# Depthwise taps of 128 channels moved from VectorE to TensorE as 32x32 diagonal tiles, with a new order of issue

## The chip, the core and the metric

The kernel runs on one NeuronCore of a Trainium2 chip. Its engines work side by side and are synchronised by semaphores: TensorE (matmuls, PE in the profile; PEld is its weight loading), VectorE (DVE), ScalarE (ACT), GpSimd (POOL) and SyncE (SP, which here only issues DMAs). Here each engine's instructions are given in a fixed order by the program. Matmuls read the on-chip memory SBUF and write PSUM; VectorE and ScalarE read both.

The metric is the time of one execution on the device in microseconds, the median of several runs. The profile is one execution, recorded instruction by instruction.

## What is computed

64 images of 96 channels by 56x56 pixels pass through a convolution block, a Fourier attention and a feed-forward part. Cut to what matters here (`bn` are folded batch norms):

```python
# convolution block, per image
out = silu(bn(einsum('bchw,oc->bohw', x, expand_w)))          # 96 -> 192 channels
out = channel_shuffle(shift_groups(out), groups=4)             # each quarter shifted by one pixel
dw  = bn(conv(out, dw_w, 3x3, feature_group_count=192))        # depthwise: 9 taps a channel
idb = bn(out * id_w)
out = silu(bn(dw + idb))
se  = sigmoid(grouped_1x1(relu(grouped_1x1(mean(out)))))       # one gate a channel
out = silu(bn(einsum('bchw,oc->bohw', out * se, proj_w)) + x)  # 192 -> 96, plus x
# attention on tokens t = [3136, 96]
h = relu(bn(layernorm(t) @ w1.T))
X = fft(h, axis=tokens); xr, xi = relu(...X...), relu(...X...)
t = t + bn(ifft(xr + 1j * xi).real @ w2.T)
# feed-forward in 8-bit floats
t = t + qlinear(relu(qlinear(layernorm(t), W1, b1)), W2, b2)
```

A depthwise tap multiplies every pixel of a channel by one number of that channel and adds it, shifted by up to one pixel, to the result. All nine taps of the 192 channels are the work that the change moves.

## The kernel before

The 192 middle channels lie in two arrays: `e_a` holds 128 channels of the whole image, one channel a partition; `e_b` holds the other 64 channels twice, the upper half of the image in partitions 0 to 63 and the lower half in 64 to 127. A depthwise pass `i` covers 28 rows: 0 and 1 are the halves of `e_a`, 2 is all of `e_b`. Every tap is one VectorE instruction over 128x1568 numbers:

```python
    x_buf = [const.tile([CP, PAD, PAD], F32, name=f"x_{i}") for i in range(2)]
    t_buf = [const.tile([CP, NPIX + 8], F32, name=f"t_{i}") for i in range(2)]
    # ... (cut)
    d_buf = const.tile([128, 3 * HH, HW], F32, name="d")

    def depthwise(b, i):
        # ... (cut)
        h, r0 = divmod(i, 2)
        e = e_b if h else e_a
        dst = d_buf[:, i * HH : (i + 1) * HH, :]
        for n, tap in enumerate((4, 0, 1, 2, 3, 5, 6, 7, 8)):
            dy, dx = divmod(tap, 3)
            win = e[:, dy + r0 * HH : dy + r0 * HH + HH, dx : dx + HW]
            w = taps[:, h, tap : tap + 1]
            if n == 0:
                nc.vector.tensor_scalar(dst, win, w, None, ALU.mult)
            else:
                nc.vector.scalar_tensor_tensor(dst, win, w, dst, ALU.mult, ALU.add)
            yield

    def mid_silu(b, i, cvs):                       # ScalarE, with the sums for the gates
        # ... (cut)
        nc.scalar.activation(
            dst, dst, AF.Silu, bias=mid_b[:, i // 2 : i // 2 + 1], accum_out=cvs[b][:, i : i + 1]
        )
        yield

    def project(b, cvs):
        # ... (cut)
        for j in range(HW // PJ):                  # 8 groups of 7 rows
            # ... (cut)
            ps = psb.tile([CP, PJ, HW], F32, tag="psb", name="ps_pj")
            nc.tensor.matmul(ps, lhsT=eye, rhs=xi[:, ...], start=True, stop=False)            # adds x
            nc.tensor.matmul(ps, lhsT=pw[:, 0, :], rhs=d_buf[:, r0 : r0 + PJ, :], start=False, stop=False)
            nc.tensor.matmul(
                ps, lhsT=pw[:, 1 + half, :], rhs=d_buf[:, HW + rb : HW + rb + PJ, :], start=False, stop=True
            )
            nc.scalar.activation(tv[:, :, r0 : r0 + PJ], ps.rearrange("p a b -> p b a"), AF.Silu, bias=pj_sh)
            yield
        if b + 2 < NB:
            load_x(b + 2)

    def deviations(b):                             # of the layer norm before the attention
        def squares(g):
            cen = psb.tile([C, 4 * CP], F32, tag="psb", name="ps_c")
            nc.tensor.matmul(cen, lhsT=center, rhs=t[:, g * 4 * CP : (g + 1) * 4 * CP], start=True, stop=True)
            sqs[g] = work.tile([C, 4, CP], F32, tag="sq", name="sq")
            nc.scalar.activation(sqs[g], cen.rearrange("p (k f) -> p k f", f=CP), AF.Square)
        def variances(g):
            # ... (cut)
            for k in range(4):
                nc.tensor.matmul(var[:, k : k + 1], lhsT=sq[:, k, :], rhs=mean_m, start=True, stop=True)
            nc.vector.tensor_scalar(v[:, js], var, 1e-5, None, ALU.add)
            nc.gpsimd.tensor_tensor(rs[:, js], v[:, js], mhalf[0:CP, 0:4], ALU.pow)
        # ... (cut)
```

PSUM is split into two pools: `psa`, two tiles of two banks for the attention, and `psb`, four tiles of one bank for everything else.

The order of issue is worked out as the program is built. The attention of image b (`mixing`, with six stages: `ps_w` from `w1`, `ps_f` twice, `ps_w` from `w2`, `ps_i` twice) is the main line. Between its steps the other parts ("sides") are put in: the feed-forward of image b-1, and the convolution of images b+1 and b+2. `PLAN` says at which points of the main line, in units of its own, a side begins and ends:

```python
PLAN = {
    "mixing": (22.3, 18.0, 30.7, 18.0, 12.0, 23.2),
    "ffn": (0.0, 63.5),
    "expand_a": (1.2, 20.0),
    "depthwise_2": (8.4, 36.3),
    # ... (cut)
    "excitation": (42.0, 44.0),
    "project": (60.0, 86.0),
    # ... (cut)
    "deviations": (87.0, 110.4),
    "silu_1": (115.9, 118.2),
}
```

The first two images' convolution is done part after part ahead of the first attention.

## Time and profile before

Three runs took 9521.79, 9529.6 and 9544.45 us. The profiled execution has a span of 9482.8 us.

| | busy us | share of the span |
|---|---|---|
| TensorE, matmuls | 8133.7 | 86% |
| VectorE | 6389.5 | 67% |
| ScalarE | 4790.4 | 51% |
| GpSimd | 2240.6 | 24% |

| operation | us of one, mean | count |
|---|---|---|
| tap, `scalar_tensor_tensor` on 128x1568 | 1.85 | 1536 |
| silu of a pass, 128x1568 | 1.61 | 192 |
| projection matmul, 128x392 (each recorded twice) | 0.49 a record | 3072 records |
| silu of the projection, 112x392 | 0.62 | 512 |
| load of half of x, 588 KB, to landing | 8.3 (median) | 128 |

The granted TensorE clock averages 0.898 of full speed. How to read the profile: lines of the kernel are given as L with a number; `out<-in` are the program's names of what an instruction writes and reads. A float32 matmul is recorded as two matmuls and two weight loads. The recorded lengths of matmuls overlap, because they are pipelined, so the distance from start to start is the better measure. In the list of waits each line reads: who waited, for whom, how long in total, how often, and the longest. A wait put down to "issue" is time in which an engine waited for nothing that the profile shows.

### The profile page before, as it was taken

What the parts mean: (1) busy time and instruction counts of PE and PEld (TensorE: products, weight loads), DVE (VectorE), ACT (ScalarE), POOL (GpSimd) and SP (SyncE); (2) the same over time, 40 slices, a digit from 0 to 9 for tenths busy, and PEclk for the clock granted to TensorE, in tenths of its full rate; (3) what the DMA queues carried; (4) which work ended last, traced back from release to release, by engine and by line L of the source; (5) the groups of instructions that cost most, each with busy time, mean ns of one, the idle gap of its engine ahead of it and who ended that gap; (6) DMA issues with size and microseconds to landing.
All of it is one profiled execution on the core that took longest, in us unless ns stands there. A gap on an engine that the chain in (4) does not pass through costs nothing.

```text
span 9482.8 us, 263604 instructions
## 1 busy us (share of the span) xinstructions
PE 8133.7 (86%) x118530; PEld 6030.7 (64%) x118530; DVE 6389.5 (67%) x9034; ACT 4790.4 (51%) x9099; POOL 2240.6 (24%) x1360
## 2 busy tenths in 40 slices
PE   5888888888888888888888888888888888888887
PEld 3666666666666666666666666666666666666666
DVE  6667666666666766676666766666666666676764
ACT  2455454454554545545545545455455454554545
POOL 0222222222222222222222222222222222222221
PEclk8988999898888999999989989889998898888988
DMA  2111111111101111111111111111110111111100
GB/s 40 17 22 16 19 21 16 20 17 17 22 15 19 17 19 21 17 18 21 17 17 22 16 19 18 17 21 17 17 22 14 20 17 17 22 16 19 18 13 15
DMA packets 411399, 177.45 MB, mean 19 GB/s; under 512 B 366323, under 2 KB 409707, under 8 KB 410011
## 3 DMA queue, kind: packets, MB, share of 16 engines
q1 hardware_dynamic: 408508, 155.59, 13.0%
q8 instruction: 930, 15.24, 0.7%
q10 hardware_dynamic: 1264, 3.48, 0.1%
q0 software_dynamic: 496, 1.50, 0.1%
q14 instruction: 201, 1.64, 0.1%
HBM read 82.62 MB, written 77.07 MB: 17 GB/s over the span
## 4 chain that ended last, share of the span: by engine, by line
PE 67%; DVE 13%; ACT 9%; issue 6%; POOL 5%; DMA 0%; POOLq 0%; ACTq 0%; DVEq 0%
PE ps_f L490 8%; PE ps_i L608 7%; PE ps_c L417 5%; PE ps_i L590 5%; POOL rs L650 5%; PE ps_v L426 4%; PE ps_w L468 4%; PE ps_pj L395 4%; PE ps_w L555 4%; PE ps_pj L396 4%; PE ps_pj L397 3%; DVE d L343 3%; PE ps_f L524 3%; ACT h L684 3%; DVE buf_h L475 3%
## 5 line engine op out<-in xcount | busy, mean ns | idle before, releaser
L343 DVE SCALAR_TENSOR_TENSOR d<-e_a,taps,d 128x1568 f32<-128x1568 f32 x1024 | 1892.0, 1848 | 14.3
L428 POOL TENSOR_TENSOR rs<-v,mhalf 112x4 f32<-112x4 f32 x448 | 1060.1, 2373 | 2650.7 <-DVE v L427 2589.6
L700 POOL TENSOR_TENSOR o<-t,o 112x448 f32<-112x448 f32 x448 | 587.6, 1312 | 2921.7 <-DVE o L698 2921.7
L650 POOL TENSOR_TENSOR rs<-v,mhalf 112x4 f32<-112x4 f32 x448 | 582.8, 1301 | 1637.1 <-DVE v L649 1637.1
L343 DVE SCALAR_TENSOR_TENSOR d<-e_b,taps,d 128x1568 f32<-128x1568 f32 x512 | 943.4, 1843 | 0.5
L427 DVE TENSOR_SCALAR v<-ps_v 112x4 f32<-112x4 f32 x448 | 72.0, 161 | 1281.0 <-PE ps_v L426 1270.3
L490 PEld LDWEIGHTS ps_f<-f_tab,buf_h 128*64 128x64 f32 x24576 | 747.3, 138 | 163.5 <-DVE buf_h L475 57.2
L490 PE MATMUL ps_f<-f_tab,buf_h 128*64 128x58 f32 x24576 | 797.8, 223 | 40.0 <-DVE buf_h L475 40.0
L676 ACT CAST y<-ps_h 128x448 f16<-128x448 f32 x1344 | 723.9, 539 | 148.8 <-PE ps_h L674 130.2
L684 ACT CAST h<-y 128x448 fp8e5<-128x448 f16 x1344 | 770.4, 573 | 0.3 <-DVE y L681 0.3
L681 DVE TENSOR_SCALAR y<-y,qb 128x448 f16<-128x448 f16 x1344 | 649.1, 487 | 154.6 <-ACT y L676 135.4
L590 PE MATMUL ps_i<-inv_tab,buf_g 112*32 112x56 f32 x24576 | 482.4, 253 | 285.7 <-issue 284.8
L468 PE MATMUL ps_w<-w1c,t 112*64 112x96 f32 x14336 | 708.0, 250 | 0.0
L468 PEld LDWEIGHTS ps_w<-w1c,t 112*64 112x64 f32 x14336 | 611.6, 137 | 139.3 <-issue 117.0
L426 PEld LDWEIGHTS ps_v<-mean_m,sq 96*112 96x112 f32 x3584 | 516.2, 213 | 281.4 <-issue 257.2
L608 PE MATMUL ps_i<-r_tab,buf_h 64*64 64x56 f32 x14336 | 676.1, 276 | 1.0 <-ACT buf_h L597 1.0
L590 PEld LDWEIGHTS ps_i<-inv_tab,buf_g 112*32 112x32 f32 x24576 | 439.1, 139 | 339.8 <-issue 293.0
L608 PEld LDWEIGHTS ps_i<-r_tab,buf_h 64*64 64x64 f32 x14336 | 647.9, 189 | 5.0 <-ACT buf_h L597 1.1
L475 DVE SCALAR_TENSOR_TENSOR buf_h<-ps_w,rs_full 128x768 f32<-128x768 f32 (+1 forms) x512 | 437.3, 854 | 254.8 <-PE ps_w L468 245.8
L690 PE MATMUL ps_o<-h,q 128*112 128x448 fp8e5 x1344 | 421.3, 393 | 213.1 <-ACT h L684 213.0
L597 ACT COPY buf_h<-ps_i 128x896 f32<-128x896 f32 x192 | 174.0, 906 | 787.8 <-PE ps_i L590 787.8
L417 PE MATMUL ps_c<-t,center 112*96 112x448 f32 x896 | 553.2, 706 | 11.6 <-issue 10.9
(159 smaller groups left out, 14740.5 us busy)
## 6 DMA issues: line engine op xcount, KB each, us to landing
x<-in_x SPq DMA_DIRECT2D x128, 588.0 KB, 8.3
out_dram<-o SPq DMA_DIRECT2D x896, 84.0 KB, 1.9
l_tab<-in_tab_l ACTq DMA_DIRECT2D x1, 1624.0 KB
r_tab<-in_tab_r ACTq DMA_DIRECT2D x1, 1568.0 KB
t<-dev_t SPq DMA_DIRECT2D x64, 7.0 KB, 1.8
t<-dev_t SPq DMA_DIRECT2D x64, 5.2 KB
ex_row_p<-in_expand_row POOLq DMA_DIRECT2D x1, 336.0 KB, 4.2
s_p<-in_bn POOLq DMA_DIRECT2D x1, 288.0 KB, 4.0
```

The costliest lines, as they stand in the source:

```text
L343: nc.vector.scalar_tensor_tensor(dst, win, w, dst, ALU.mult, ALU.add)
L417: nc.tensor.matmul(cen, lhsT=center, rhs=t[:, g * 4 * CP : (g + 1) * 4 * CP], start=True, stop=True)
L426: nc.tensor.matmul(var[:, k : k + 1], lhsT=sq[:, k, :], rhs=mean_m, start=True, stop=True)
L428: nc.gpsimd.tensor_tensor(rs[:, js], v[:, js], mhalf[0:CP, 0:4], ALU.pow)
L468: nc.tensor.matmul(ps[hc * 64 : hc * 64 + 64, k, 0:C], lhsT=t[:, n0 : n0 + 64], rhs=w1c[:, hc * C : hc * C + C], start=True, stop=True,)
L475: nc.vector.scalar_tensor_tensor(h_v[:, :, d * NJ + j0 : d * NJ + j0 + n], ps[:, 0:n, 0:C].rearrange("p b c -> p c b"), 0.0, rs_full[:, d, ...
L490: nc.tensor.matmul(ps[r * 64 : r * 64 + 64, k, 0 : 2 * NK], lhsT=buf_h[:, n0 : n0 + 64], rhs=f_tab[:, r, :], start=True, stop=True,)
L590: nc.tensor.matmul(ps[p0 : p0 + 32, k, 0:HW], lhsT=u_v[:, oh * 48 + o, :], rhs=inv_tab[:, r, :], start=True, stop=True,)
L608: nc.tensor.matmul(ps[pr, bk, k, 0:HW], lhsT=buf_h[pr, n2 * 48 : n2 * 48 + 64], rhs=r_tab[pr, n2, :], start=True, stop=True,)
L650: nc.gpsimd.tensor_tensor(rs, v, mhalf[0:CP, 0:4], ALU.pow)
L676: nc.scalar.copy(y16, ps)
L684: nc.scalar.copy(held[i // 3][:, i % 3, :], held.pop(("y", i)), saturate=False)
```

## The change

The taps of the 128 channels of `e_a` become matmuls with diagonal weights: for each tap and each group of 32 channels a 32x32 matrix with the taps on its diagonal. The 128x128 array is used as 16 tiles. Row tile r reads channels 32r to 32r+31; column tile j works on another group of seven rows of the image. The four row tiles write four different PSUM banks, so half an image (four row groups) takes all four `psb` tiles, and the nine taps are summed in PSUM. ScalarE then applies the silu out of PSUM. The taps of `e_b` stay on VectorE. The purpose is to take work off VectorE and to use a TensorE array that has idle parts in such small products.

After that, a partition of `d_buf` holds 32 channels of one row group, so the projection is done in row tiles of 32 rows, four at a time, with the `e_b` part in two row tiles of 64. The identity matmul that added x is replaced by an addition on VectorE in PSUM. The variances of the layer norm take the form used in the feed-forward part: pixels on partitions, and a reduction on VectorE in place of matmuls with a column of 1/96. There is one x buffer (two before) and there are three t buffers (two before). A single schedule orders all images; a side that holds all four `psb` tiles keeps others out until it is done ("hold"), and cannot start within the first part of the feed-forward ("part").

```diff
 PLAN = {
-    "mixing": (22.3, 18.0, 30.7, 18.0, 12.0, 23.2),
-    "ffn": (0.0, 63.5),
-    "expand_a": (1.2, 20.0),
...
+    "mixing": (16.9, 18.0, 30.0, 18.0, 12.0, 19.7),
+    "ffn": (112.9, 176.9),
+    "expand_a": (-139.2, -120.0),
+    "expand_b": (-114.4, -95.4),
+    "depthwise_0": (-118.2, -110.2),
+    "depthwise_1": (-100.1, -97.9),
+    "last_taps": (-97.5, -76.2),
+    "last_silu": (-89.9, -63.3),
+    "excitation": (-71.5, -57.0),
+    "project": (-66.5, -42.2),
+    "deviations": (-40.0, -17.7),
 }
...
+    def depthwise(b, i, cvs):
...
+        pss = [psb.tile([128, PJ, HW], F32, tag="psb", name="ps_d") for _ in range(4)]
+        for tap in range(9):
+            dy, dx = divmod(tap, 3)
+            for j in range(4):
+                r0 = start_row(i, j) + dy
+                for r in range(4):
+                    pr = slice(r * 32, r * 32 + 32)
+                    nc.tensor.matmul(
+                        pss[r][j * 32 : j * 32 + 32],
+                        lhsT=diag[pr, tap, :],
+                        rhs=e_a[pr, r0 : r0 + PJ, dx : dx + HW],
+                        start=tap == 0,
+                        stop=tap == 8,
+                    )
+            if tap % 3 == 2:
+                yield "hold"
+        for r in range(4):
+            nc.scalar.activation(
+                d_buf[:, i, r], pss[r], AF.Silu, bias=mid_b[:, r : r + 1], accum_out=sums[:, i * 4 + r : i * 4 + r + 1]
+            )
+        yield
...
     def project(b, cvs):
...
+        for i in range(2):
+            pss = [psb.tile([CP, PJ, HW], F32, tag="psb", name="ps_pj") for _ in range(4)]
+            for g in range(4):
+                for j in range(4):
+                    pr = slice(j * 32, j * 32 + 32)
+                    nc.tensor.matmul(pss[j], lhsT=pw[pr, g, :], rhs=d_buf[pr, i, g], start=g == 0, stop=False)
+                if g == 1:
+                    yield "hold"
+            for j in range(4):
+                pr = slice(j % 2 * 64, j % 2 * 64 + 64)
+                r0 = (2 * i + j // 2) * PJ
+                nc.tensor.matmul(pss[j], lhsT=pw[pr, 4, :], rhs=d_last[pr, r0 : r0 + PJ, :], start=False, stop=True)
+            yield "hold"
+            for j in range(5):
+                if j < 4:
+                    r0 = start_row(i, j)
+                    nc.vector.tensor_tensor(
+                        pss[j], pss[j], xi[:, r0 + 1 : r0 + 1 + PJ, 1 : HW + 1], ALU.add
+                    )
+                if j:
...                      # silu of row group j - 1 into t, on ScalarE
+                yield None if j == 4 else "hold"
+        load_x(b + 1)
...
         def squares(g):
-            cen = psb.tile([C, 4 * CP], F32, tag="psb", name="ps_c")
-            nc.tensor.matmul(cen, lhsT=center, rhs=t[:, g * 4 * CP : (g + 1) * 4 * CP], start=True, stop=True)
...
+            cen = psb.tile([CP, 4, 128], F32, tag="psb", name="ps_c")
+            for k in range(4):
+                n0 = (g * 4 + k) * CP
+                nc.tensor.matmul(cen[:, k, 0:C], lhsT=t[:, n0 : n0 + CP], rhs=center, start=True, stop=True)
...
         def variances(g):
-            for k in range(4):
-                nc.tensor.matmul(var[:, k : k + 1], lhsT=sq[:, k, :], rhs=mean_m, start=True, stop=True)
...
+            nc.vector.tensor_reduce(v[:, js], sqs.pop(g), AX.X, ALU.add)
...
     # feed-forward: the second product of a row group is issued one step later
-            j, m = divmod(i - 5, 3)
-            if i >= 5 and m == 0 and j < NCH:
+            j, m = divmod(i - 6, 3)
+            if i >= 6 and m == 0 and j < NCH:
                 second(j)
...
+    # what a side waits for: (part, how many images back, steps)
+    SIDES = {
+        "expand_a": (7, (("project", 1, None),)),
+        "depthwise_0": (4, (("expand_a", 0, None),)),
+        "last_taps": (9, (("expand_b", 0, None),)),
+        "project": (14, (("excitation", 0, None), ("ffn", NT, None))),
+        "deviations": (10, (("project", 0, None), ("mixing", 1, 8))),
...
```

The times in the new plan count from the start of the image's own attention, so -139.2 lies in the attention of image b-2. The gate now also uses a form that needs no halving, and the excitation takes nine sums in place of three.

## The prediction

> **What bounds the kernel now.** I read the engines' shares first, then the stretches, the waits of TensorE, the groups of the parts that change, and last a timeline of one period. The page and the stretch from 1000 to 9000 us (busy time of each engine, then granted clock):
>
> ```profile
> PE 8133.7 (86%) x118530; PEld 6030.7 (64%) x118530; DVE 6389.5 (67%) x9034; ACT 4790.4 (51%) x9099; POOL 2240.6 (24%) x1360
> PE 67%; DVE 13%; ACT 9%; issue 6%; POOL 5%; DMA 0%; POOLq 0%; ACTq 0%; DVEq 0%
> ...
> 1000.00:9000.00 8000.00, 6950.09 (x101502) 5155.75 (x101503) 5445.07 (x7692) 4102.07 (x7797) 1931.86 (x1153) 0.90 0.14 18
> ```
>
> TensorE is busy 86.9% of the stretch. The first matmul of the attention stage (the first `ps_w` of each image) returns every 146.7 us (median of 63 distances). So one image costs 127.4 us of busy TensorE, 99.8 of VectorE, 75.2 of ScalarE; TensorE idles 19.2 us. The second line, the chain that ended last, shows the same: TensorE two thirds, VectorE next. What TensorE waits for (total us, times, longest):
>
> ```profile
> PE ps_i L590 <- issue: 284.8, 55, 5.9
> PE ps_dev L434 <- DVE dev L432: 229.1, 128, 3.2
> PE ps_o L690 <- ACT h L684: 213.0, 272, 1.5
> PE ps_x L665 <- DVE xt L656: 175.8, 199, 2.0
> PE ps_se L372 <- ACT red L367: 146.5, 64, 2.3
> ```
>
> Divided by 64: 4.4, 3.6, 3.3, 2.7 and 2.3 us an image. Those on `dev` and `xt` come from VectorE's queue, where one tap holds 1.85 us:
>
> ```profile
> L343 DVE SCALAR_TENSOR_TENSOR d<-e_a,taps,d 128x1568 f32<-128x1568 f32 x1024 | 1892.0, 1848 | 14.3
> L343 DVE SCALAR_TENSOR_TENSOR d<-e_b,taps,d 128x1568 f32<-128x1568 f32 x512 | 943.4, 1843 | 0.5
> L341 DVE TENSOR_SCALAR d<-e_a,taps 128x1568 f32<-128x1568 f32 x128 | 131.8, 1030 | 11.1 <-PE ps_pj L396 7.7 <-ACT e_a L298 3.4
> L648 DVE TENSOR_REDUCE v<-sq 112x4 f32<-112x384 f32 x448 | 243.8, 544 | 23.8 <-ACT sq L641 23.8
> L618 DVE SCALAR_TENSOR_TENSOR t<-ps_i,bn2c_b,t 112x392 f32<-112x392 f32 x512 | 296.3, 620 | 159.0 <-PE ps_i L608 157.3
> ```
>
> The timeline (start, length, engine, line) gives what a float32 matmul costs; each is recorded as two:
>
> ```profile
> 4081.47 0.96 PE L297 MATMUL ps_ea<-x,ex_w 112*32 112x448 f32 x8
> ...
> 4005.55 1.52 PE L312 MATMUL ps_eb<-x,ex_b 112*32 112x392 f32 x16
> ...
> 4014.27 0.82 PE L396 MATMUL ps_pj<-d,pw 128*112 128x392 f32 x2
> 4014.93 0.82 PE L397 MATMUL ps_pj<-d,pw 128*112 128x392 f32 x2
> ...
> 4052.29 2.02 PE L590 MATMUL ps_i<-inv_tab,buf_g 112*32 112x56 f32 x74 [5.15 <-issue]
> ```
>
> A full-width matmul of 392 columns takes 0.66 us from start to start. Four in four column tiles (`ps_ea`, 448 columns) take 0.9 us together, eight of `ps_eb` in two rounds 1.46 us: 0.73 us for a round of four. Within a round the records start 6 to 7 ns apart. The last line shows the stall put down to "issue": 5.15 us with nothing to wait for, 10 us after the two loads of x (588 KB each) were issued at 4037.51. I take it that TensorE's own instructions arrive late behind those loads; the profile does not prove it.
>
> **What the Trainium skill says.** "TensorE: Matmul & The Clock Gate", Part 3 (packing small matmuls), gives 10.6x for 16 tiles of 32x32 at 512 columns, tiles starting some 4 ns apart. The trace agrees as far as it goes: four column tiles side by side, and two row tiles of 64 (`ps_w` from `w2b`: eight matmuls of 96 columns in 0.96 us, 0.12 each, against 0.195 for full-height ones). Sixteen appear nowhere in it. "TensorEngine Tiling (Array Packing)", Restrictions and Gotchas, wants different row tiles in different PSUM banks; the change does that, which is why one depthwise step takes four `psb` banks. Its Key Properties say a change of tiling drains TensorE; here that is the 0.1 to 0.15 us by which a batch's first interval is longer. Part 1 of the first page says the array's clock falls after idle windows; the trace grants 0.90, and the same eight `ps_ea` records take 1.72 us at 175.49 and 0.96 at 178.89.
>
> **The change, part by part, us per image.**
> VectorE loses the taps of the first 128 channels: (1892.0+131.8)/64 = -31.6. It gains eight additions of x, at the 0.62 of the like-sized `t` update +5.0, and seven reductions at 0.544 (+3.8). 99.8 becomes 77.
> ScalarE: two silus of 1.61+0.19 become eight of about 0.5+0.19 (`e_b`, 392 columns from PSUM, takes 0.498): +1.9; the rest cancels. 75 becomes 77.
> TensorE, from busy time by tile in the same stretch (us of 8000, divided by 54.5 images):
> 1. Old projection, 926.2: -17.0.
> 2. Variances: `ps_c` 469.8 and `ps_v` 397.6 go, -15.9. The new form is that of `ps_n` in the feed-forward part, 390.2: +7.2.
> 3. Taps: 2 halves x 9 taps x 16 matmuls of 392 columns. If 16 tiles run together, a tap is one round: 18 x 0.73 = 13.1.
> 4. New projection: per half, 16 matmuls of 32 rows in four row tiles (4 rounds) and 4 of 64 rows in two (2 rounds); 12 x 0.66 = 7.9, with drains 8.5. The identity matmul that added x is gone.
> Sum: 127.4 - 17.0 - 15.9 + 7.2 + 13.1 + 8.5 = 123.3. TensorE's work shrinks by only 4 us; the larger gain must come from its idle time.
>
> Idle, 19.2 now. `dev` 3.6 -> 1: the plan puts the remaining taps (-97.5 to -76.2) where no deviations (-40.0 to -17.7) run. `xt`, with the smaller releasers of `ps_x`, 3.2 -> 2: those taps come after the first part of the feed-forward. `ps_o` 3.3 -> 0.5: it is issued one step later. `ps_se` 2.3 -> 0.5: four steps spread over 14 units instead of 2. Issue 4.4 -> 3: x is now loaded in the middle of the `ps_w` stage, whose instructions are sparser than those of `ps_i`. Remainder 1.5. New: two depthwise halves and two projection halves each need all four `psb` banks empty and keep the other side work out; I put 1.5 us on each, 6 in all. Sum 14.5.
>
> Period 123.3+14.5 = 137.8, 8.9 less. The mean of the 63 periods is 1% under the median now, so 63 x 136.4 = 8593. Before the first period: 172.7 us now, of which two images' taps fill much; with one image at the start I expect 115. After the last start 157 now, 155 then. 8863 in the profile; measured times lie 0.5% above it (9529.6 against 9482.8): 8907. The plan's own period falls from 124.2 to 114.6, 7.7%; applied to 145.3 this gives 63 x 134.1 + 270 = 8718, or 8760 measured. I take 8840.
>
> **Rivals.**
> A. Sixteen tiles do not overlap, only four: 72 rounds x 0.73 = 52.6 instead of 13.1. TensorE 163, period 177, total about 11,500. For it: no such pattern in the trace. Against: four column tiles and two row tiles do overlap, and records can follow at 6.5 ns, so 32 fit in a round. 6%.
> B. The four-bank holds cost 4 to 5 us each, not 1.5: every hold waits for the last evictions of other work and ends behind four silus in ScalarE's queue. Idle is then 26, period 149, total about 9600. Against: attention has its own two PSUM buffers and can fill the gap. 8%.
> C. The single x, e and d buffers make the convolution a closed loop: expand to projection spans 97 of the plan's 114.6 units, at 1.2 us a unit 116 us, plus 10 us for loading x: 126. Under 138, but with 12 us of slack; were it exceeded, the period would be set there, at 140 to 145, total 9000 to 9300. 12%.
> D. Everything fits better than I allow, idle 8 us, and a busier TensorE keeps a higher clock: period 129, total about 8400. 15%.
>
> **Range and chances.** 8840, 8450 to 9300 for eight in ten: the low end is near D, the high end takes in most of C. Over 2% faster means under 9339: all but A, B and a little of C, 0.88. Within 2% 0.05, slower 0.07.
>
> **What would show it.** TensorE busy about 123 us an image; 16-tile rounds of 0.66 to 0.75 us; VectorE near 77; the wait on `dev` gone; projection near 8.5. Wrong if a tap round takes over 1 us (A), if `ps_d` and `ps_pj` wait for ScalarE over 10 us an image (B), or if `ps_ea` waits for x (C).

## The result and the profile after

| | before | after | ratio to before |
|---|---|---|---|
| median time, us | 9525.7 (9517.7 to 9544.5, 4 runs) | 9241.4 (9232.7 to 9243.3, 4 runs) | 0.9697, interval 0.968 to 0.9714 |
| profiled span, us | 9482.8 | 9238.1 | |
| period of the first `ps_w`, us (median) | 146.7 | 143.0 | |
| TensorE busy in a period, us | 127.4 | 126.9 | |
| VectorE busy in the span | 67% | 52% | |

The change gains 3.0%, 284 us; I had forecast 8840, a gain of about 690. The profiled spans differ by 245 us: 63 periods that are 3.4 us shorter in the mean (211), a start shorter by 27 (with the convolution of one image ahead of the first attention, in place of two) and a tail shorter by 6. Two lines of the page of the changed kernel (engines' shares; the chain that ended last) and the stretch from 1000 to 9000 us (busy time of each engine, then granted clock):

```profile
PE 8110.8 (88%) x159362; PEld 6129.3 (66%) x159362; DVE 4801.2 (52%) x8793; ACT 4804.3 (52%) x9806; POOL 1771.3 (19%) x1360
...
PE 72%; ACT 13%; DVE 9%; issue 5%; DMA 0%; POOL 0%; ACTq 0%; POOLq 0%; SPq 0%; DVEq 0%
...
1000.00:9000.00 8000.00, 7099.70 (x139856) 5371.24 (x139851) 4167.61 (x7622) 4200.86 (x8582) 1548.95 (x1176) 0.94 0.14 19
```

VectorE has lost a quarter of its work and its share of the chain has fallen from 13% to 9%; TensorE's has risen from 67% to 72%. The granted clock has risen from 0.90 to 0.94. What TensorE waits for (total us, times, longest):

```profile
PE ps_se L406 <- ACT red L400: 335.4, 64, 5.8
PE ps_h L726 <- ACT y L728: 143.8, 66, 2.3
PE ps_i L644 <- issue: 126.2, 56, 4.4
PE ps_x L719 <- DVE xt L710: 104.8, 73, 1.8
PE ps_o L744 <- ACT h L738: 98.3, 124, 1.7
```

The wait on `dev` is gone from the list. The one on `red`, 2.3 us an image before, stands first with 5.2. The groups of the parts that changed (busy us, mean ns of one, idle before):

```profile
L359 PE MATMUL ps_d<-e_a,diag 32*32 32x392 f32 x36864 | 1040.5, 497 | 0.0
L382 DVE SCALAR_TENSOR_TENSOR d_last<-e_b,taps,d_last 128x1568 f32<-128x1568 f32 x512 | 954.1, 1864 | 12.6 <-ACT e_b L334 9.9
...
L438 PE MATMUL ps_pj<-d,pw 32*112 32x392 f32 x4096 | 470.6, 506 | 33.8 <-DVE pw L421 32.7 <-ACT t L454 0.6
...
L480 DVE TENSOR_REDUCE v<-sq 112x4 f32<-112x384 f32 x448 | 247.7, 553 | 1011.6 <-ACT sq L476 1006.6
...
L444 PE MATMUL ps_pj<-d_last,pw 64*112 64x392 f32 x1024 | 201.5, 512 | 0.0
```

Divided by 64: taps on TensorE 16.3 us an image, projection 10.5, taps left on VectorE 14.9 without the first, and 3.9 for the reductions that VectorE has gained (3.8 forecast).

Where in the image the time went is seen when a period is cut at the first matmul of each attention stage (medians; us, TensorE's busy part behind the slash):

| stage, by its matmuls | before | after |
|---|---|---|
| first product, `ps_w` from `w1c` | 30.7 / 26.6 | 39.7 / 36.5 |
| first Fourier product, `ps_f` from `f_tab` | 17.6 / 16.6 | 16.3 / 15.8 |
| second Fourier product, `ps_f` from `l_tab` | 36.2 / 31.1 | 41.1 / 31.4 |
| second product, `ps_w` from `w2a` | 18.8 / 18.8 | 13.3 / 13.3 |
| inverse, `ps_i` from `inv_tab` | 24.1 / 18.7 | 16.0 / 12.7 |
| inverse, `ps_i` from `r_tab` | 19.2 / 15.6 | 16.6 / 16.6 |

The taps on TensorE went into the first and the last row, the expand of the last 64 channels (6.3 us) from the third into the first. The projection, of which 8.1 us lay in the third row and 8.8 in the fourth, now lies wholly in the third (10.2 us). Idle time of TensorE fell from 14 to 7 us in the other five stages together and rose from 5 to 10 us in the second Fourier product. The timeline of that stage in one image (start, length, engine, line):

```profile
5010.85 2.45 PE L578 MATMUL ps_f<-l_tab,buf_g 128*64 128x112 f32 x28
...
5013.23 0.61 PE L396 MATMUL ps_se<-sums,rd_w 128*24 128x1 f32 x18
...
5017.69 0.68 ACT L593 ACTIVATE ue<-ps_f,fb 128x392 f32<-128x392 f32 x1 [0.53 <-DVE buf_h L677]
...
5018.27 0.24 ACT L400 ACTIVATE red<-ps_se,rd_b 24x1 f32<-24x1 f32 x1
...
5018.56 0.60 PE L406 MATMUL ps_se<-red,ep_w 24*32 24x1 f32 x32 [4.72 <-ACT red L400]
...
5020.55 3.09 PE L572 MATMUL ps_f<-l_tab,buf_g 128*128 128x112 f32 x16
...
5025.06 3.47 PE L438 MATMUL ps_pj<-d,pw 32*112 32x392 f32 x32 [0.85 <-DVE pw L421]
...
5028.46 1.57 PE L444 MATMUL ps_pj<-d_last,pw 64*112 64x392 f32 x8
...
5029.97 1.37 PE L572 MATMUL ps_f<-l_tab,buf_g 128*128 128x112 f32 x10
...
5031.27 3.81 PE L438 MATMUL ps_pj<-d,pw 32*112 32x392 f32 x32
```

`red` is a quarter of a microsecond of work, but ScalarE reaches it 4.4 us after `ps_se` is done: ahead of it in the queue stand feed-forward casts and a `ue` that waits for VectorE's `buf_h`. Behind the pause sixteen `ps_f` take 3.09 us in place of 2.0: the granted clock is 0.5 from 5016.1 to 5023.0. Then come ten microseconds of projection, with the last group of the stage between its two halves. The stage has a crowded front of ScalarE and VectorE and a back that is TensorE's alone.

### The profile page after: what moved, and what is told of

The parts are those of the page before. It is cut to its first block, busy times and chain, and to the rows that moved or that the text cites. A ratio compares the mean times of both kernels' runs of the same rounds, so it can differ in the third digit from the quotient of the medians.

```text
span 9238.1 us, 345738 instructions
## 1 busy us (share of the span) xinstructions
PE 8110.8 (88%) x159362; PEld 6129.3 (66%) x159362; DVE 4801.2 (52%) x8793; ACT 4804.3 (52%) x9806; POOL 1771.3 (19%) x1360
## 3 DMA queue, kind: packets, MB, share of 16 engines
q1 hardware_dynamic: 408682, 155.77, 13.3%
q8 instruction: 1248, 20.45, 1.0%
q14 instruction: 204, 1.67, 0.1%
## 4 chain that ended last, share of the span: by engine, by line
PE 72%; ACT 13%; DVE 9%; issue 5%; DMA 0%; POOL 0%; ACTq 0%; POOLq 0%; SPq 0%; DVEq 0%
PE ps_d L359 11%; PE ps_w L522 7%; PE ps_f L544 6%; PE ps_pj L438 5%; PE ps_i L662 5%; PE ps_c L474 5%; PE ps_w L609 4%; PE ps_n L693 4%; PE ps_ea L309 4%; PE ps_i L644 4%; PE ps_eb L323 4%; ACT h L738 3%; ACT ue L593 3%; PE ps_w L621 3%; ACT y L728 2%
## 5 line engine op out<-in xcount | busy, mean ns | idle before, releaser
L754 POOL TENSOR_TENSOR o<-t,o 112x448 f32<-112x448 f32 x448 | 862.5, 1931 | 3417.9 <-ACT h L738 1686.8
L359 PE MATMUL ps_d<-e_a,diag 32*32 32x392 f32 x36864 | 1040.5, 497 | 0.0
L382 DVE SCALAR_TENSOR_TENSOR d_last<-e_b,taps,d_last 128x1568 f32<-128x1568 f32 x512 | 954.1, 1864 | 12.6 <-ACT e_b L334 9.9
L704 POOL TENSOR_TENSOR rs<-v,mhalf 112x4 f32<-112x4 f32 x448 | 451.5, 1008 | 2496.8 <-DVE v L703 2496.8
L369 ACT ACTIVATE d<-ps_d,mid_b 128x392 f32<-128x392 f32 x512 | 294.0, 586 | 1202.9 <-PE ps_d L359 1202.9
L359 PEld LDWEIGHTS ps_d<-e_a,diag 32*32 32x32 f32 x36864 | 627.6, 103 | 298.2 <-issue 49.2
L572 PEld LDWEIGHTS ps_f<-l_tab,buf_g 128*128 128x128 f32 x3712 | 597.3, 247 | 274.9 <-DVE o L752 158.4
L482 POOL TENSOR_TENSOR rs<-v,mhalf 112x4 f32<-112x4 f32 x448 | 447.2, 1009 | 1514.5 <-DVE v L481 1497.6
L672 DVE SCALAR_TENSOR_TENSOR t<-ps_i,bn2c_b,t 112x392 f32<-112x392 f32 x512 | 296.8, 621 | 674.9 <-PE ps_i L662 674.9
L572 PE MATMUL ps_f<-l_tab,buf_g 128*128 128x112 f32 x3712 | 616.0, 334 | 35.1 <-ACT buf_g L553 30.0
L726 PE MATMUL ps_h<-xq,q 96*128 96x448 fp8e5 x1344 | 447.6, 377 | 154.9 <-ACT y L728 143.8
```

What stands on the lines that cost most here:

```text
L359: nc.tensor.matmul(pss[r][j * 32 : j * 32 + 32], lhsT=diag[pr, tap, :], rhs=e_a[pr, r0 : r0 + PJ, dx : dx + HW], start=tap == 0, stop=tap ...
L382: nc.vector.scalar_tensor_tensor(d_last, win, w, d_last, ALU.mult, ALU.add)
L572: nc.tensor.matmul(ps[:, k, 0:CP], lhsT=g_v[:, k1, 0:128], rhs=l_tab[:, k1, :], start=True, stop=True)
L754: nc.gpsimd.tensor_tensor(o32, tv[:, rows, :], o16, ALU.add)
```

## Experiments

Each starts from the changed kernel unless it says otherwise. Ratios are to the kernel before, measured beside it; 0.9697 is that of the change. "us an image" is the period, or the difference of two times divided by 64.

### What a tap on TensorE costs

**One tap instead of nine.** Eight of nine taps of the first 128 channels are left out.

```diff
-            for j in range(4):
+            for j in range(4) if tap == 4 else ():
...
-                        start=tap == 0,
-                        stop=tap == 8,
+                        start=True,
+                        stop=True,
```

> Leaves out eight of the nine taps that TensorE does for the first 128 channels (only the centre tap is computed); everything else is as in the changed kernel. Theory 1, TensorE is the bound and its tap rounds are what eats the gain: the taps are 16.4 us of busy TensorE an image, so 8/9 of that, 14.6 us, goes, and the time falls by 64 x 12 to 64 x 14.6 = 770 to 930 us, to 8310 to 8470. Theory 2, the stretch from the second Fourier product on is bound by the alternation of ScalarE and VectorE and the taps lie in time that is free anyway: under 300 us, 8940 or more. Theory 3, the single x, e and d buffers close a loop that sets the period: the loop gets shorter by the same 14.6 us, so the time falls as in theory 1, but TensorE then idles over 20 us an image.

8274.0 us, 0.8703 (0.8687 to 0.8718): 967 us less, 15.1 an image, 36 us more than the first theory allowed. The stretch from 1000 to 8000 us, to be read like the one above:

```profile
1000.00:8000.00 7000.00, 6162.09 (x108539) 4745.87 (x108539) 4085.37 (x7474) 4125.34 (x8404) 1521.06 (x1155) 0.94 0.16 21
```

TensorE is still 88% busy: busy time fell by 14.2 us an image (126.9 to 112.7), the time by 15.1. It idles 15.3 us of a period of 128.0, not over 20, so the third theory is out. The first product falls from 39.7 to 29.3 us, the last stage from 16.6 to 12.1, the second Fourier product stays at 41.1. So the taps lie in stages that TensorE bounds and cost their full length; next to nothing hides them.

**Another order of the sixteen tiles**, row groups outside, column groups inside.

```diff
-            for j in range(4):
-                r0 = start_row(i, j) + dy
-                for r in range(4):
+            for r in range(4):
+                for j in range(4):
+                    r0 = start_row(i, j) + dy
```

> Within a tap the column tiles run fastest in place of the row tiles; the same 16 matmuls. In the changed kernel the first tap of a half takes 0.69 us and each later one 0.87. Theory 1, matmuls are dealt out in the order of the program, a tile holds one running and one waiting half product, and the dealer stands still once a tap until the first tile is free, then needs 0.19 us to start again: the order does not matter, 0.87 us a tap, and the time stays within 30 us of 9241. Theory 2, weight loads of one row tile wait for products of the same row tile: the order matters; if the tap then takes 0.70 us, 3 us an image go and the time falls by about 190 us to 9050; if it takes 1.1 us the time rises by about 250 us.

9197.5 us, 0.9675 (0.966 to 0.9689), 44 us under the change where the first theory allowed 30, in an interval that overlaps with that of the change. A batch of nine taps takes 7.46 us from first to last start, 7.47 before. Which of the two tile indices runs fastest does not set the length of a round.

**Short taps.** 168 columns in place of 392; four of seven rows of these channels are left out, also in their silu.

```diff
-                        pss[r][j * 32 : j * 32 + 32],
+                        pss[r][j * 32 : j * 32 + 32, 0:3],
...
-                        rhs=e_a[pr, r0 : r0 + PJ, dx : dx + HW],
+                        rhs=e_a[pr, r0 : r0 + 3, dx : dx + HW],
```

> The taps of the first 128 channels on TensorE with 3 of 7 rows, 168 instead of 392 columns (leaves the other rows of these channels out, also in their silu). In the changed kernel the first tap's round takes 0.69 us and each later one 0.87. Theory 'a fixed standstill of some 0.2 us for each later round, the rest in proportion': first round 0.30 to 0.36, later ones 0.48 to 0.55. Rival 'all in proportion': later ones 0.37 to 0.40. Rival 'a floor by the number of matmuls or weight loads of a round (32 records)': 0.6 to 0.87. Time, 18 rounds an image shorter by 0.35 us: 400 us less at the first theory, about 8850.

8977.7 us, a single time and 128 above the 8850 of the first theory; `ps_d` waits on "issue" for 123.7 us in all here. Two lines on the tile `ps_d`, of the changed kernel and of this one (ns of one recorded half: shortest, median, longest):

```profile
L359 PE MATMUL ps_d<-e_a,diag x36864: 484/487/516, 57.0 to 8995.2; 32*32 32x392 f32 x200
```

```profile
L360 PE MATMUL ps_d<-e_a,diag x36864: 297/300/328, 57.1 to 8735.9; 32*32 32x168 f32 x200
```

224 columns less shorten a half by 0.187 us, so a matmul of two halves by 0.374: 1.67 ns a column, as full-width ones show (0.66 us for 392). In batches of nine taps that no other work interrupts (65 of the 128 in the changed kernel), the distance from the start of a round to that of the next is 0.68 us, then 0.78, then 0.84 with 392 columns; with 168 it is 0.35, then 0.53, then 0.47 to 0.48 until the first interruption. The 0.87 of the expectations is the mean distance between the last records of the rounds, which counts the slow start of the second round too. Less the streaming, 0.66 and 0.28, a steady round has an excess of 0.18 and 0.19 to 0.20 us: it does not shrink with the columns, and "all in proportion" is out.

What makes the excess is not shown. Two lengths fit the fixed standstill of the first theory. They also fit a limit by the number of records once a batch is under way: in the first round records start 6.7 ns apart, in later ones mostly 16 to 17 ns, and 32 of those are 0.53 us, more than the whole short round. A third length would have to separate the two.

### What VectorE and the gate cost

**More VectorE work in the taps.** After each of the last eight taps four of half size go into a spare tile.

```diff
                 nc.vector.scalar_tensor_tensor(d_last, win, w, d_last, ALU.mult, ALU.add)
+                for h in (0, HH // 2, 0, HH // 2):
+                    half = win[:, h : h + HH // 2, :]
+                    nc.vector.scalar_tensor_tensor(d_spare, half, w, d_spare, ALU.mult, ALU.add)
```

> VectorE gets back the load that it lost: beside each of eight taps of the last 64 channels stand four more instructions on half-sized operands into a spare tile, about 31 us an image; nothing reads the result. Theory 1, VectorE's relief is what shortened TensorE's waits: the waits for VectorE come back and the time rises by 5 us an image or more, over 9560. Theory 2, VectorE has room now and only its place in the order matters: the time rises by less than 100 us (under 9340).

11228.4 us, 1.181 (1.1793 to 1.1828), 31.0 us an image for 34.0 us of work (2048 instructions of 1.06 us over 64 images). The first Fourier product grows from 16.3 to 30.5 us, the second from 41.1 to 58.1, no other stage grows. TensorE now waits here:

```profile
PE ps_h L731 <- ACT y L733: 650.3, 252, 5.1
PE ps_o L749 <- ACT o L751: 431.8, 129, 5.7
```

VectorE is busy for 52% of the span of the changed kernel, but for 14.3 of the 16.3 us and 31.8 of the 41.1 us of the two stages where the plan puts these taps. That leaves 11.3 us of room, and not all of it can be used.

**Eight of nine VectorE taps left out.**

```diff
-            else:
+            elif tap < 0:
                 nc.vector.scalar_tensor_tensor(d_last, win, w, d_last, ALU.mult, ALU.add)
```

> Leaves out eight of the nine VectorE taps of the last 64 channels, 8 x 1.85 = 14.8 us of VectorE an image, which the plan puts in the first and second Fourier products. Theory 'VectorE is on the path there' (from 31 us added, which cost 31): the second Fourier product gets shorter by 6 to 10 us (then ScalarE, at 31 us of work, or TensorE, at 31, bounds it), the time is 8600 to 8850. Rival 'the alternation of ScalarE and VectorE and the feed-forward casts bind, the taps only fill VectorE's gaps': under 2 us an image, 9120 to 9240.

9169.9 us, 0.9646 (0.9614 to 0.9678): 1.1 us an image for 14.9 us of work taken away. The second Fourier product goes from 41.1 to 40.2. Here the first theory fell: what hurts when added need not help when removed. But the edit reaches less far than its expectation says: of the 15.9 us of taps 12.1 lie in the first Fourier product, where TensorE is busy 15.8 of 16.3 us and little can be gained, and only 3.9 in the second, which became 0.9 us shorter.

**The gate's steps spread out.**

```diff
-    "excitation": (-71.5, -57.0),
+    "excitation": (-79.0, -55.0),
```

> The excitation's four steps are put from -79.0 to -55.0 in the plan in place of -71.5 to -57.0, so that its relu stands earlier in ScalarE's queue and other TensorE work stands between the two small products. Theory 1: TensorE's wait for that relu (5.3 us an image) is a wait of its own; it falls below 1 us and the time falls by 200 to 340 us, to 8900 to 9040. Theory 2: the stage is bound by the alternation of ScalarE and VectorE, and the wait moves to the next product that needs a ScalarE result: the wait on the relu falls, others grow, and the time changes by less than 60 us (9180 to 9300).

9266.7 us, 0.9748 (0.9731 to 0.9764). The time lies where the second theory had it, but the wait on `red` is 342.9 us against 335.4. The edit did not do what it was for: in either kernel the second product of the gate follows the first on TensorE with nothing between them, in all 64 images, and `red` starts 5.5 us after the first (the kernel before has one record between them in 62 of 64 images, and `red` after 2.8 us). So this run says nothing on what an earlier `red` would bring.

**No gate.** The projection reads constant weights; `ps_se`, `red`, tanh and `pw` are left out.

```diff
-        sums = cvs[b]
-        ps = psb.tile([128, 8], F32, tag="psb", name="ps_se")
...
-        cvs[b] = pw
-        yield
+        for _ in range(4):
+            yield
+        cvs[b] = pj_w
```

> Leaves out the squeeze-and-excitation gate altogether (no ps_se, red, ps_se2, tanh, pw; the projection reads its constant weights). In the changed kernel TensorE waits 335 us in all (5.3 us an image) for red in ScalarE's queue, where I had forecast 0.5. Theory 'the wait is the cost': those 4.8 us an image come off, some 300 us, so about 8940. Theory 'the wait is a symptom' (the second Fourier product is bound by what ScalarE and VectorE have to do there, and TensorE has to stand still somewhere): the idle time turns up as waits of ps_f, ps_h or ps_o instead, the stage stays at 40 to 41 us, and the time is between 9180 and 9240.

9235.0 us, 0.9712 (0.9679 to 0.9745): nothing. The largest wait of the profile was worth no time that can be measured. The second Fourier product takes 39.5 us in half of the images and 41 to 43 in most others: 40.5 in the mean, against 40.9. TensorE's list of waits in this run:

```profile
PE ps_o L714 <- ACT h L708: 240.8, 251, 1.9
PE ps_h L696 <- ACT y L698: 144.2, 66, 2.3
PE ps_i L614 <- issue: 138.8, 64, 4.3
PE ps_x L689 <- DVE xt L680: 104.9, 73, 1.8
PE ps_pj L408 <- ACT o L716: 89.0, 62, 2.0
```

Much of the 335 us has come back as waits of `ps_o` on `h` (98 to 241), `ps_pj` on `o` (89) and `ps_f` on `ue` (50).

**The VectorE taps in the first product**, where VectorE is busy 14.9 of 39.7 us.

```diff
-    "expand_a": (-139.2, -120.0),
-    "expand_b": (-114.4, -95.4),
+    "expand_a": (-136.2, -117.0),
+    "expand_b": (-139.2, -122.2),
...
-    "last_taps": (-97.5, -76.2),
+    "last_taps": (-119.0, -97.7),
```

> Same work: in the plan expand_b goes ahead of expand_a and the VectorE taps go to -119.0 to -97.7, that is into the first matmuls (ps_w from w1c), where TensorE is busy 36.6 of 39.7 us and VectorE only 14.9. If the taps cost time because of where they stand, the second Fourier product falls from 41 to 33-36 us while the first stage keeps its 39.7, and the time falls to 8750 to 8950; also 17 us less before the first attention. Rival 'the place does not matter, the sum of the waits stays' : 9180 to 9260.

10020.6 us, 1.0539 (1.0505 to 1.0572), a clear miss of both theories. The second Fourier product falls to 39.0 us only; it had held just 3.9 us of the taps. The last stage, with more of the expand in it, grows from 16.6 to 20.2, and the first product from 39.7 to 48.9, though 6.5 us of expand have left it, with this wait, 104.8 us in the changed kernel:

```profile
PE ps_x L719 <- DVE xt L710: 688.5, 312, 3.3
```

In this stage the feed-forward normalises (`xt`) on VectorE, and each tap ahead of an `xt` in the queue holds it up for 1.86 us. The edit also changed the order of the two expands, so the 3.6 us of the last stage can come from that. A stage in which an engine is a third busy is no free place for long instructions if short ones there stand in TensorE's chain.

### What sets the second Fourier product

**Feed-forward spread over the period.**

```diff
-    "ffn": (112.9, 176.9),
+    "ffn": (112.9, 224.9),
```

> Same work: the feed-forward of an image is spread over 112 instead of 64 units of the plan's period, so its ScalarE and VectorE instructions also fall into the three last attention stages, where both engines are under half busy. If the second Fourier product is long because ScalarE and VectorE are crowded there, it falls from 41 to 34-37 us, the last three stages grow by 0 to 3, and the time falls to 8850 to 9050. Rival 'TensorE-bound stages pay for it' (ps_x, ps_h and ps_o wait in stages that have no idle time now): 9200 to 9400.

9871.7 us, 1.0386 (1.0346 to 1.0426). ScalarE has 27.1 us of work in the stage instead of 30.9, and the stage stays at 41.3. The second half of the depthwise, kept out by the longer first part of the feed-forward, goes from the first product (28.6) to the first Fourier product (27.4), which comes out even; but what was moved lengthens the three stages behind by 10.4 us, two of which had no gap in TensorE before.

**`ue` as two tiles.**

```diff
-            ue = work.tile([128, 2, 8, HW], F32, tag="ue", name="ue")
+            ue = [work.tile([128, 8, HW], F32, tag=tag, name="ue") for tag in ("ue", "ue1")]
...
-                a = ue[:, q, 0:n, :]
+                a = ue[q][:, 0:n, :]
```

> Same work: in the second Fourier product the tile ue with its two halves (q = 0, 1) becomes two tiles of half the size, so ScalarE's second ue need not wait for VectorE's last read of the first. In both profiles that chain, ScalarE ue, VectorE s, VectorE ue, and again, takes 5.7 to 5.8 us for each of the six groups with hardly a gap, about 35 of the 41 us of the stage. Theory 'this alternation bounds the stage, and so no wait taken away there counts': a group falls to 4.5 to 5 us, the stage to 34-37, the period by 4 to 7 us: 8800 to 8990. Rival 'ScalarE's and VectorE's sum of work, with the feed-forward casts, bounds it': the queue is in order and full, the stage keeps 39 to 41 us, 9150 to 9240.

9186.9 us, 0.9646 (0.9631 to 0.966): 0.5% under the change, the intervals apart, so a version that beats both kernels. But the stage is 40.0 us, and ScalarE's wait for VectorE's `ue` is still there, 175.1 us against 152.5. The edit did not take away what it was to take away. The Trainium skill, "PSUM — Partial Sum Buffer", section "PSUM bank collisions raise a hardware error", wants any two engines kept apart in one bank and 32-partition quadrant, reads too; both halves of `ue` are made from the same `ps_f`, whose real part ScalarE reads and whose imaginary part VectorE reads. That would explain the wait; no run here isolates it.

**Pair order.** ScalarE makes both halves of `ue`, then VectorE both of `s`, then both of `ue`.

```diff
             for q in range(2):
-                nc.scalar.activation(a, re, ...)
-                nc.vector.scalar_tensor_tensor(s[:, q, 0:n, :], im, par[:, m : m + 1], a, ALU.mult, ALU.add)
-                nc.vector.scalar_tensor_tensor(a, im, par[:, 4 + m : 5 + m], a, ALU.mult, ALU.add)
-                yield M_F2 / 20
+                nc.scalar.activation(ue[:, q, 0:n, :], re, ...)
+            for dst, c in ((s, 0), (ue, 4)):
+                for q in range(2):
+                    m = 1 - q
+                    nc.vector.scalar_tensor_tensor(
+                        dst[:, q, 0:n, :], im, par[:, c + m : c + m + 1], ue[:, q, 0:n, :], ALU.mult, ALU.add
+                    )
+                yield M_F2 / 20
```

> Same work, another order in the second Fourier product: ScalarE makes both halves of ue first, then VectorE both of s, then both last ones of ue; so VectorE's four operations follow each other without ScalarE in between. Theory 'the alternation bounds the stage': a group falls from 5.75 us to what VectorE needs, 4 x 0.69 + 2 x 0.55 + casts and taps, about 4.6 to 5.2; the stage from 41 to 34-37 us, the time to 8800 to 9000. Rival 'TensorE's order in the stage (projection halves of 5 us and the feed-forward between the groups) bounds it': 39 to 41 us, 9150 to 9240.

9241.5 us, 0.9724 (0.968 to 0.9767), stage 41.7 us. The alternation is gone and nothing is gained. With eight VectorE taps left out as well:

> The same, and eight of the nine VectorE taps left out (14.8 us of VectorE an image). With the old order leaving them out gave 70 us. If they only filled VectorE's gaps in the alternation, they cost more once the alternation is gone: another 150 to 400 us below the pair order with the taps. If TensorE or ScalarE bounds the stage then, again under 100 us.

9139.9 us, 0.9618 (0.9582 to 0.9653), stage 40.2: 102 us for the taps instead of 71, near the rival. In the kernel before, the same order:

> The pair order in the kernel before the change. Its second Fourier product takes 36.2 us with the same 5.75 us a group. Theory 'the alternation is the same bound in both kernels and the change left it alone': 2 to 5 us an image less, 9200 to 9400, ratio 0.965 to 0.985. Rival: there VectorE is at 67% and its taps bind, 9450 to 9550.

9659.1 us, 1.0171 (1.0128 to 1.0214): 1.3 to 2.1% longer, and its stage goes from 36.2 to 38.9. To take the alternation away in this form gains nothing in either kernel; whether the new order brings a cost of its own is not shown.

**The feed-forward's 8-bit casts on VectorE.** Its bias and relu writes 8 bits at once; one rounding is left out.

```diff
-            nc.vector.tensor_scalar(y16, y16, qb1[:, i % 3 : i % 3 + 1], 0.0, ALU.add, ALU.max)
...
-            nc.scalar.copy(held[i // 3][:, i % 3, :], held.pop(("y", i)), saturate=False)
+            nc.vector.tensor_scalar(
+                held[i // 3][:, i % 3, :], held.pop(("y", i)), qb1[:, i % 3 : i % 3 + 1], 0.0, ALU.add, ALU.max, saturate=False
+            )
```

> In the feed-forward the cast of the hidden values to 8 bits (21 ScalarE casts of 0.57 us an image, 12.0 us) goes away: VectorE's bias and relu writes the 8-bit values at once, without the rounding to 16 bits between, so one rounding is left out. ScalarE 75 -> 63 us an image. Theory 'ScalarE's queue is the bound in the first Fourier product and the first 24 us of the second': the stage falls from 41 to 33-37 us, the wait of ps_se on red from 5.3 to under 3 us an image, the time to 8750 to 9000. Rival 'once ScalarE is relieved the alternation or VectorE (with its taps) binds at once': 39 to 41 us, 9120 to 9240.

9244.5 us, 0.9707 (0.9672 to 0.9741), though ScalarE's work in the stage falls from 30.9 to 24.6 us: stage 41.5, the wait on `red` 376 us. With the pair order too:

> The same, with the pair order of ue (ScalarE both, then VectorE four). If ScalarE's queue alone bounds: the same as the cast alone, within 60 us. If two bounds of the same length lie behind each other: the stage at 31 to 34 us, 8600 to 8850, while each alone gives under 120 us.

9244.8 us, 0.971 (0.9681 to 0.9739), stage 42.1. ScalarE's queue alone is not the bound either.

**All four**: pair order, casts on VectorE, no gate, one VectorE tap of nine.

> The pair order and the casts on VectorE, and left out besides: the gate (the projection reads its constant weights) and eight of the nine VectorE taps. Each alone gave 0 to 1.6 us of the 41 of the second Fourier product. Theory 'four bounds of nearly one length beside each other': together they free the stage down to TensorE's own work, 31 us; stage 31 to 34, period 133 to 136, 8550 to 8800. Rival 'another thing sets it': 38 us or more, above 9000.

9001.4 us, 0.9464 (0.9435 to 0.9493). The stage is 38.2 us (median) and the time 9001, both just inside the rival's limits. By the means over the images, which serve better here because the stage takes several lengths, each alone had taken 0.9 (taps), 0.4 (gate), -0.4 (pair) and -0.4 us (casts) off the stage of 40.9; together 3.1, not the 7 to 10 of four bounds beside each other. Another 20 us of the 240 are in the start, which needs no gate and few taps here. TensorE in the stage of one image:

```profile
4487.98 1.56 PE L548 MATMUL ps_f<-l_tab,buf_g 128*64 128x112 f32 x28 [1.22 <-DVE ue L566]
4489.47 0.90 PE L715 MATMUL ps_o<-h,q 128*112 128x448 fp8e5 x3
4493.73 3.10 PE L542 MATMUL ps_f<-l_tab,buf_g 128*128 128x112 f32 x16 [3.36 <-DVE ue L566]
...
4501.59 4.39 PE L408 MATMUL ps_pj<-d,pj_w 32*112 32x392 f32 x26 [2.79 <-ACT o L717]
...
4507.41 1.37 PE L542 MATMUL ps_f<-l_tab,buf_g 128*128 128x112 f32 x10
```

It now waits for one of the two `ps_f` buffers, which VectorE frees with its last `ue` (279 us in the whole run), and for a fourth `psb` bank before the projection can go on (129 us on `o`). In the changed kernel the waits of `ps_f` on `ue` were 7 us, and its list has no wait of TensorE's projection on `o`.

**Projection behind the stage.**

```diff
-    "project": (-66.5, -42.2),
-    "deviations": (-40.0, -17.7),
+    "project": (-50.0, -37.0),
+    "deviations": (-35.0, -15.0),
```

> Same work: the plan moves the projection from -66.5..-42.2 (two halves of 5 us of TensorE, the first ahead of the sixth group of the second Fourier product) to -50..-37, behind that stage, and the deviations to -35..-15. In the changed kernel the sixth group's alternation starts 4 us late behind the first half. Theory 'the projection stretches the stage because it stands between two links of its chain': the stage falls from 41 to 33-36, the next (18.8 before, 13.3 after) grows by 5 to 10 us of projection that has to be done anyway and that now lies beside nothing; net 0 to -3 us an image, 9050 to 9240. Rival 'the hold behind four silus and the load of x, now closer to the next expand, cost more than is gained': ps_ea waits for x or ps_ea and ps_c for banks, 9300 to 9600.

9810.6 us, 1.0302 (1.0286 to 1.0317). No other single edit shortens the stage so much: 41.1 to 33.5 us. The second product, though, grows from 13.3 to 22.7, the inverse from 16.0 to 21.5 and the last stage from 16.6 to 18.1. Of the 8.9 us that an image loses, 3.6 are waits of `ps_i` and `ps_c` on "issue" (153 to 385 us), 1.6 a wait of `ps_w` on `ue`, and 1.9 are TensorE's own busy time, while the time at half clock rose from 1125 to 1660 us. Loads of x and the stall behind them, changed kernel:

```profile
5039.94 3.12 SPq L117 DMA_DIRECT2D x<-in_x  x2
...
5055.38 0.49 PE L644 MATMUL ps_i<-inv_tab,buf_g 112*32 112x56 f32 x9 [3.87 <-issue]
```

and here, where the load follows the later projection:

```profile
4927.35 2.88 SPq L117 DMA_DIRECT2D x<-in_x  x2
...
4942.89 1.91 PE L644 MATMUL ps_i<-inv_tab,buf_g 112*32 112x56 f32 x72 [5.84 <-issue]
```

Stalls of over 2.5 us of `ps_i` or `ps_c` within 25 us of a load: 54 in the kernel before (median 5.4 us), 31 in the changed one (3.7), 62 here (6.1). They begin 9, 11 and 9 us after the load.

The DMA packets in the traces show what ends them. TensorE's instructions arrive in packets of 16 KB, 1248 in the changed kernel for 319,578 records of TensorE, 256 to a packet. Each of the 54, 31 and 62 stalls begins at the same place in this count of 256; exactly one such packet is under way in it, and TensorE goes on 1.2 to 1.6 us after its landing (medians 1.37, 1.34 and 1.36). So TensorE had run out of instructions. Within 14 us of a load such a packet takes 1.76 us (median), elsewhere 1.06; that it also starts late, 2.3, 0.4 and 2.9 us into the stall, is measured but not explained.

With `ue` split as well:

> Both edits together. If alternation and projection both stretch the second Fourier product: the stage at 28 to 33 us, then bound by TensorE's own work, and 8650 to 8900. If only the split counts: the same as with the split alone, within 60 us. If only the place of the projection counts: the same as with that alone.

9749.8 us, 1.0232 (1.0215 to 1.0249): the split gives 61 us here and 55 without; the two edits add up.

## Why the prediction was wrong

The direction held, and so did much of the mechanism: sixteen tiles overlap (rival A out), VectorE fell to 74.5 us an image (77 forecast), ScalarE to 75.1 (77), the `dev` wait went, the four-bank holds cost about 1.2 us rather than 6 (rival B out), and `ps_ea` waits for x 5.6 us in the whole run (no sign of rival C). The size did not hold. The 401 us between 8840 and 9241 come from these steps:

| step, us an image | forecast | measured |
|---|---|---|
| taps on TensorE | 13.1 | 16.4 |
| new projection | 8.5 | 10.3 |
| variances | 7.2 | 7.3 |
| `ps_i`, `ps_f`, `ps_se`, taken as unchanged | 43.7 | 41.1 |
| TensorE busy in all | 123.3 | 126.9 |
| idle: `ps_se` on `red` | 0.5 | 5.2 |
| idle: `ps_h`, `ps_o`, `ps_x` | 2.5 | 6.2 |
| idle: issue, `dev` | 4 | 2.4 |
| idle: holds (`ps_n` on d, `ps_pj` on pw) | 6 | 1.2 |
| idle in all | 14.5 | 16.1 |
| period | 137.8 | 143.0 |

The mean period is 141.9 us against 136.4: 63 x 5.5 = 346 us. The start took 145.5 us instead of 115 (+30): the last expand of image 0 goes behind its second depthwise half, so eight of its nine VectorE taps run only from 83 us on and TensorE stands for 17. The tail gave 4 back. Measured times no longer lie 0.5% above the profile (-41). The remaining 67 are the step from 8907 to 8840, towards the plan's own ratio; it was the wrong way.

**The step that failed first is the tap term, "18 x 0.73 = 13.1".** The mechanism was right and the size off. I took 0.73 from `ps_eb`, two rounds in four column tiles; sixteen tiles used nine times in a row take 0.68 us once, 0.78 once and 0.84 after that, and with the ends of the batches 16.4 us an image. One tap instead of nine showed that this time counts in full; the other order and the short taps, that the excess is neither a matter of the order nor in proportion to the columns. What makes it stays open. The projection was 1.8 us short in a like way: its later rounds in four row tiles do run at 0.66, with sums into the same banks, but the first of a half takes 0.76 or 0.94, and each half ends with a `d_last` part of 1.57 us where two rounds at 0.66 had been put.

**The second is "Idle": waits taken off a sum one by one**, `ps_se` 2.3 to 0.5, `ps_o` 3.3 to 0.5. Its total was off by only 1.6 us, but by luck: holds and issue were set too high, `ps_se` and `ps_h` too low. That the gate's steps are spread over 14 units of the plan put nothing between its two products on TensorE, so the second waits the whole time for `red`. Removing the gate shows the fault of the sum: 5.2 us of wait, no time. In the second Fourier product TensorE stands about 10 us of 41. The new plan took 6.3 us of `ps_eb` out of this stage and put the second half of the projection in, and more of the stage ran at half clock: `ps_f` from `l_tab` costs 13.4 us an image in place of 11.7, 5.9 of them at half clock in place of 2.4. So TensorE's work in the stage stayed at 31 us while its pauses doubled. Only the projection moved out again made the stage short (33.5 us), and cost more elsewhere.

**What helped unseen**: the half clock. Time at half clock fell from 1938 to 1125 us of the span, `ps_i` from 18.3 to 13.7 us an image at the same work, with 12.5 and 1.7 us of it at half clock. Counted at full clock (busy time less half of what lay in stretches at half clock) TensorE's work rose, from 115.4 to 120.3 us an image, where I had its busy time fall by 4. Why the clock was granted more is not shown.

What remains open is which loop sets the front of the second Fourier product. Gate, alternation and casts, and the 3.9 us of taps that lie there, each bring under 1 us alone and 3.1 of 10 us together; the two `ps_f` buffers with VectorE's last read, and TensorE's fixed order with the projection in it, are what is left. A third `ps_f` buffer was not tried. Nor was the variance form alone, so the gain is not split by parts.

## What to carry to other kernels

Moving work from an engine that is not the bound to the one that is pays only if as much leaves the latter: here TensorE took 16 us of taps, got rid of about as much, and gained from fewer waits and a higher granted clock. A wait in the list is a symptom until a run without it says otherwise; before subtracting one, ask what the same engine would wait for next. Price a packed round from repeated rounds on the same tiles, and look at a stage's own share of each engine, and at what short instructions stand in its queues, before calling it a free place.

## What the runs showed that I had not expected

- Sixteen-tile rounds of float32 matmuls, repeated on the same tiles, take 0.84 us with 392 columns and 0.47 to 0.48 with 168, some 0.2 us over 1.67 ns a column. The Trainium skill, "TensorE: Matmul & The Clock Gate", Part 3, gives one matmul plus 4 ns for each further tile; the first round agrees in kind (0.68 us, halves 6.7 ns apart), the later ones do not.
- The "issue" stalls after a load of x are TensorE waiting for its own instructions: all 147 of them, in three kernels, end 1.2 to 1.6 us after a 16 KB packet of instructions has landed.
- 34.0 us added to a 52% busy VectorE cost 31.0; 14.9 taken away gave 1.1. A share over the span says little: 12.1 us of these taps lay in a stage that TensorE fills, 3.9 in the one with gaps.
